# A graph layer with sorted messages: a stated opening order, a small first table, clears in long runs, and blocks stored in pairs

## The chip, the cores and the metric

The kernel runs on one core of a Trainium2 chip. The metric is the device time of one execution in microseconds. Three runs of the kernel before took 1536.56, 1531.3 and 1529.97, median 1531.3.

## The reference

There are 6250 nodes with 128 features, and 100,000 edges, each with a source, a destination and 128 features of its own. The destinations are sorted, the sources are random.

```python
msg_in = jnp.concatenate([x[row], x[col], edge_attr], axis=-1)
h = msg_in @ W + b
# h = layernorm(h) * gamma + beta
msg = jax.nn.relu(h)
out = jax.ops.segment_sum(msg, row, num_segments=x.shape[0])
x = _layernorm(x + out)
```

`row` is the source, `col` the destination. So messages are summed by the random index, and the sorted one is only looked up.

## The kernel before, in words

W has three parts: one for the source, one for the destination, one for the edge. The source and destination parts are computed once per node ("projections", `project(g, k)`, lines 219 to 248, groups of four times 128 nodes): `k = 0` gives xa, kept in SBUF, `k = 1` gives xb, written to the DRAM table xb_d. Both are kept as three bf16 parts that sum to the float32 value.

The edges are cut into 782 tiles of 128, and the tiles into three splits (260, 260, 262). Every edge is assigned to one of 50 blocks by its source (source modulo 50). Each split has a DRAM buffer `sorted`, in which each block has 6 x 128 rows of 132 floats. The work is:

1. **Placement**, `places` (lines 256 to 305). For a chunk of T tiles DVE compares the block numbers with 0 to 49 (L264, 50 x T elements), scans that along the row to count (L266), TensorE adds the counts over the partitions, DVE forms an offset per entry (L280) and a product (L281), TensorE adds both up (L287), and DVE makes `place_i`, the row to which each edge goes. Before it `source_blocks` (L174) computes block numbers from the sources.
2. **Edges**, `edges` (lines 326 to 366), in 196 slots of four tiles. SP loads the edge features eT and the destination offsets db (a pair of slots at a time, `DG = 2`) and a window of 42 rows of the table xb_d; the start row of the window is read into a register of SP (L339). DVE makes a one-hot matrix (L345), TensorE multiplies edge features and window rows (L351, L352), ACT evicts to hs (L354, eight buffers), and GpSimd (POOL) scatters 128 rows of 528 bytes per tile with an indirect DMA (L360). `windows` (L192) makes db's source, drel.
3. **Blocks**, class `Block` (lines 397 to 462), three stages for each of 3 x 50 blocks. `begin` loads the block's rows hl (L411) and makes a one-hot of the source within the block (`ohe`, L415) and its transpose (L422, L423). `middle` adds the source part (L433, L437) and computes the norm (L441 to L449). `end` sums the messages of each node (L457) into acc (L460, L462). A block needs all scatters of its split.
4. **`finish`** (L467) adds x, makes the last layer norm and writes five blocks of the output.

Rows of a block that no edge fills must hold a source number out of range. `clear` (L144) writes such rows into the last two sixths of each block, one DMA per split from ACT's queue.

The program is written in the order opening, then slots of split 0, 1 and 2; a list of side work (projections with `k = 0`, placement of the next split) is taken one by one between the slots, and the blocks of split s are taken between the slots of split s + 1, from its fifth slot on (`LAG`). The blocks of the last split follow at the end. A scheduler in the compiler then orders the instructions of each engine by its own estimate of costs; the opening is given high priority (L503). Each queue and engine runs its instructions strictly in the resulting order. The general path is for inputs that don't fit and isn't run here.

Of the kernel before, what the change touches and what calls it, by code (L numbers as in the profile page):

```python
# [15 lines left out]
P = 128  # L16
# [7 lines left out]
NB, BN = 50, 125  # L24
NPAD = 6400
PT = 4
WN = 42
PIECES = 196
# [3 lines left out]
SPLITS = [(260, 6, 4, [32, 66, 66, 66, 30]), (260, 6, 4, [65] * 4), (262, 6, 4, [66, 66, 66, 64])]  # L32
TMAX = 66
PG = 7
G = 3
# [32 lines left out]
def fast_path(ctx, tc, io, bad_d):  # L68
# [9 lines left out]
    xb_d = dram.tile([3, NPAD, D], BF16, name="xb_d")  # L78
# [10 lines left out]
    proj_pool = early.enter_context(tc.tile_pool(name="proj", bufs=2))  # L89
    src_i = setup.tile([P, TILES], I32, name="src_i")  # L90
    nc.sync.dma_start(src_i, io["srcT"])
    dst_i = setup.tile([HALF, 2, PT * P], I32, name="dst_i")
    nc.sync.dma_start(dst_i, io["dstC"])
    w3 = const.tile([P, 3, D], F32, name="w3")
    nc.scalar.dma_start(w3, io["W"].rearrange("(k p) d -> p k d", p=P))
    base_i = const.tile([1, PIECES], I32, name="base_i")
    nc.scalar.dma_start(base_i, io["base"])
# [3 lines left out]
    for t, v in ((gamma_bc, io["gamma"]), (b_bc, io["b"]), (beta_bc, io["beta"])):  # L101
        nc.scalar.dma_start(t, dram_ap(v, 0, [[0, P], [1, D]]))
# [4 lines left out]
    nc.gpsimd.iota(part_i, pattern=[[1, 1]], base=0, channel_multiplier=1)  # L107
    spare_i = setup.tile([P, TMAX], I32, name="spare_i")
    nc.gpsimd.iota(spare_i, pattern=[[P, TMAX]], base=0, channel_multiplier=1)
    ident = const.tile([P, P], F32, name="ident")  # L110
    make_identity(nc, ident)
    eps = const.tile([P, 1], F32, name="eps")
    nc.vector.memset(eps, LN_EPS)
    iota_row = const.tile([P, P], F32, name="iota_row")
# [5 lines left out]
    ones_h = const.tile([P, P], BF16, name="ones_h")  # L120
    nc.vector.memset(ones_h, 1.0)
# [16 lines left out]

    spare_rows = max(k - f for _, k, f, _ in SPLITS)
    empty = const.tile([P, spare_rows, ROW], F32, name="empty")  # L140
# [3 lines left out]
    def clear(s):  # L144
        _, k, f, _ = SPLITS[s]
        per = k - f
        return nc.scalar.dma_start(
            dram_ap(sorted_d[s], f * P * ROW, [[per * ROW, P], [k * P * ROW, NB], [1, per * ROW]]),
            row_bc(flat(empty[:, :per, :]), NB))
# [4 lines left out]
    nc.vector.tensor_scalar(sgn, gamma_bc, 0.0, 2.0, op0=ALU.is_ge, op1=ALU.mult)  # L154
    nc.vector.tensor_scalar(sgn, sgn, -1.0, None, op0=ALU.add)
    wsum = const.tile([P, 4], F32, name="wsum")
    nc.vector.tensor_reduce(wsum[:, 0:3], w3, axis=AX.X, op=ALU.add)
    nc.vector.tensor_reduce(wsum[:, 3:4], b_bc.unsqueeze(1), axis=AX.X, op=ALU.add)
    wmean = const.tile([P, 4], F32, name="wmean")
    nc.vector.tensor_scalar(wmean, wsum, 1.0 / D, None, op0=ALU.mult)  # L160
    w = const.tile([P, 3, D], F32, name="w")
    for j in (1, 2, 0):
        nc.vector.scalar_tensor_tensor(w[:, j, :], w3[:, j, :], wmean[:, j:j + 1], sgn,
                                       op0=ALU.subtract, op1=ALU.mult)
    bias = const.tile([P, D], F32, name="bias")
    nc.vector.scalar_tensor_tensor(bias, b_bc, wmean[:, 3:4], sgn, op0=ALU.subtract, op1=ALU.mult)
# [7 lines left out]
    def source_blocks(t0, t1):  # L174
        c = slice(t0, t1)
        nc.vector.tensor_copy(src_f[:, c], src_i[:, c])
        nc.vector.tensor_scalar(sloc[:, c], src_f[:, c], 0.5, 1.0 / NB, op0=ALU.add, op1=ALU.mult)
        nc.vector.tensor_scalar(sloc[:, c], sloc[:, c], -0.5, MAGIC, op0=ALU.add, op1=ALU.add)
        nc.vector.tensor_scalar(sloc[:, c], sloc[:, c], -MAGIC, None, op0=ALU.add)
        nc.vector.scalar_tensor_tensor(bkt[:, c], sloc[:, c], -float(NB), src_f[:, c],  # L180
                                       op0=ALU.mult, op1=ALU.add)
        nc.vector.tensor_copy(bkt_h[:, c], bkt[:, c])
        if t1 == TILES:
            for p0 in range(LAST, P, 32):
                nc.vector.memset(bkt_h[p0:p0 + 32, TILES - 1:TILES], 99.0)


    bad = const.tile([P, 3], F32, name="bad")
# [23 lines left out]


    xa = tabs.tile([P, NB, 3 * D], BF16, name="xa")
    acc = tabs.tile([P, NB, ACW], F32, name="acc")
    XG = 4
    n_proj = -(-NB // XG)

    def project(g, k):

        t0 = g * XG
        m = min(XG, NB - t0)
        xT = proj_pool.tile([P, XG * P], F32, name="xT", bufs=4)
        nc.sync.dma_start(xT[:, :m * P], io["xT"][:, t0 * P:(t0 + m) * P])
        ps = psum.tile([P, 4, P], F32, name="hp", bufs=2)
        for j in range(m):
            nc.tensor.matmul(ps[:, j, :], xT[:, j * P:(j + 1) * P], w[:, k, :],
                             start=True, stop=True)
        full = ps[:, :m, :]
        if k == 0:  # L230
            o = xa[:, t0:t0 + m, :]
# [3 lines left out]
        else:  # L235
            xb_t = proj_pool.tile([P, XG, 3 * D], BF16, name="xb")
            o = xb_t[:, :m, :]
        nc.scalar.copy(o[:, :, 0:D], full)
        rest_t = proj_pool.tile([P, XG, D], F32, name="rest")
        rest = rest_t[:, :m, :]  # L240
        nc.vector.tensor_tensor(rest, full, o[:, :, 0:D], op=ALU.subtract)
        nc.scalar.copy(o[:, :, D:2 * D], rest)
        nc.vector.tensor_tensor(o[:, :, 2 * D:3 * D], rest, o[:, :, D:2 * D], op=ALU.subtract)
        if k == 1:
            for i in range(3):
                nc.sync.dma_start(
                    dram_ap(xb_d, i * NPAD * D + t0 * D, [[NB * D, P], [D, m], [1, D]]),
                    o[:, :, i * D:(i + 1) * D])
# [7 lines left out]
    def places(s, t0, T):  # L256
        cap = SPLITS[s][1] * P
# [17 lines left out]
        nc.tensor.matmul(ps[:, NB:2 * NB], ones_h, cnt, start=True, stop=True)  # L275
        at = place_pool.tile([P, NB], F32, name="at")
# [4 lines left out]
        nc.vector.tensor_tensor(sc_v, sc_v, oh_v, op=ALU.mult)  # L281

        sums = psum.tile([P, 512], F32, name="pa")
        for k, (wt, v) in enumerate(((ident_h, sc_v), (ident, far_v))):
            for b in range(0, NB, PG):
# [3 lines left out]
                                 skip_group_check=True)  # L289
        pos_t = place_pool.tile([P, TMAX], F32, name="pos")  # L290
# [4 lines left out]
        nc.vector.scalar_tensor_tensor(place[:, :T], bkt[:, t0:t0 + T], float(cap), pos,  # L295
# [9 lines left out]
        nc.vector.tensor_tensor(place_i[:, t0:t0 + T], place[:, :T], other[:, :T], op=ALU.add)  # L305

# [13 lines left out]
    HS, DG = 8, 2  # L320
# [3 lines left out]
    held = {}  # L324

    def edges(s, q):
        t0 = q * PT
        m = min(PT, TILES - t0)
        if q % DG == 0:
            g = min(DG, PIECES - q)  # L330
            held["eT"] = edge.tile([P, DG * PT * P], F32, name="eT", bufs=3)
            cols = min(g * PT * P, (TILES - t0) * P)
            nc.sync.dma_start(held["eT"][:, :cols], io["eT"][:, t0 * P:t0 * P + cols])
            held["db"] = edge.tile([P, DG * PT * P], BF16, name="db", bufs=3)
            nc.sync.dma_start(held["db"][:, :g * PT * P],
                              dram_ap(drel_d, q * PT * P, [[0, P], [1, g * PT * P]]))
        c0 = q % DG * PT * P
        eT = held["eT"][:, c0:c0 + m * P]
        base = nc.values_load(base_i[0:1, q:q + 1], engines=[mybir.EngineType.SP],  # L339
                              min_val=0, max_val=N - 1,  # L340
                              skip_runtime_bounds_check_because="dst holds node numbers below N")
        win = edge.tile([P, D], BF16, name="win", bufs=6)
        nc.sync.dma_start(win[:3 * WN, :], xb_d[:, bass.ds(base, WN), :])
        oh = edge.tile([P, PT * P], BF16, name="ohd", bufs=3)
        nc.vector.tensor_scalar(oh[:, :m * P], held["db"][:, c0:c0 + m * P], part_w, None,  # L345
                                op0=ALU.is_equal)
# [7 lines left out]
        evict = nc.scalar.copy(hs[:, :m, 0:D], hp[:, :m, :])  # L354
        with tc.issue_after(evict.ins):
# [41 lines left out]
    class Block:  # L397
# [10 lines left out]
        def begin(self):  # L408
            blk, k = late["blk"], self.k
            self.hl = blk.tile([P, KMAX, ROW], F32, name="hl", bufs=4)  # L410
            nc.sync.dma_start(  # L411
                flat(self.hl[:, :k, :]),
                dram_ap(sorted_d[self.s], self.b * k * P * ROW, [[k * ROW, P], [1, k * ROW]]))
            self.ohe = blk.tile([P, KMAX, P], F32, name="ohe", bufs=3)
            nc.vector.tensor_tensor(self.ohe[:, :k, :],  # L415
                                    self.hl[:, :k, D:D + 1].to_broadcast([P, k, P]),
# [84 lines left out]
    n0 = SPLITS[0][3][0]  # L501
    parts0 = place_parts(0)
    with tc.high_priority():  # L503
        source_blocks(0, n0)
        windows()
        for g in range(n_proj):
            project(g, 1)
    parts0.pop(0)()
    source_blocks(n0, TILES)
    clear(0)  # L510
    side = parts0 + [check_windows, cuts]
    side += [lambda g=g: project(g, 0) for g in range(n_proj)]
    side += [lambda s=s: clear(s) for s in range(1, n_split)]
# [23 lines left out]
    LAG = 5  # L537
    for s, (n_tiles, _, _, _) in enumerate(SPLITS):
        p0, p1 = first_tile[s] // PT, -(-first_tile[s + 1] // PT)
        work = side if s == 0 else []  # L540
        if s + 1 < n_split:
            work = work + place_parts(s + 1)
        slots = p1 - p0
        for i in range(slots):
            edges(s, p0 + i)
            n_work = -(-len(work) // (slots - i)) if s else (1 if i % 2 == 0 or len(work) >= slots - i else 0)
            for _ in range(min(n_work, len(work))):
                work.pop(0)()
            if s == 0 and not work and not late:
# [3 lines left out]
            if s > 0 and i >= LAG:  # L553
                q0 = (i - LAG) * NB // (slots - LAG)
                q1 = (i - LAG + 1) * NB // (slots - LAG)
                for _ in range(q1 - q0):
                    step()
    check_rooms()
# [3 lines left out]
    nc.tensor.matmul(total[0:1, 0:3], ones_f, bad, start=True, stop=True)  # L562
# [257 lines left out]
```

## Time and profile before

| what | value |
|---|---|
| median of three runs | 1531.3 us |
| profiled execution | 1529.89 us |
| its span on the core | 1528.1 us |
| mean granted TensorE clock | 0.874 |
| PE, DVE, ACT, POOL busy | 76, 53, 43, 55% of the span |
| DMA in all | 238.46 MB, mean 156 GB/s |

A row of the profile's groups or timelines names the engine, the line, the operation and the tiles (written <- read). A group gives its count, busy time and mean; a timeline gives start and duration in us, and in brackets the idle time ahead of the instruction with what ended it ("issue" means that the engine waited for nothing the profile shows). In the busy slices the span is cut into 40 parts of 38.2 us, and a digit is the busy share in tenths:

```profile
POOL 0000787877878877777777777777777720000000
DVE  6999453432313425445544305545545327777766
```

### The profile page before, as it was taken

What the parts mean: (1) busy time and instruction counts of PE and PEld (TensorE: products, weight loads), DVE (VectorE), ACT (ScalarE), POOL (GpSimd) and SP (SyncE); (2) the same over time, 40 slices, a digit from 0 to 9 for tenths busy, and PEclk for the clock granted to TensorE, in tenths of its full rate; (3) what the DMA queues carried; (4) which work ended last, traced back from release to release, by engine and by line L of the source; (5) the groups of instructions that cost most, each with busy time, mean ns of one, the idle gap of its engine ahead of it and who ended that gap; (6) DMA issues with size and microseconds to landing.
All of it is one profiled execution on the core that took longest, in us unless ns stands there. A gap on an engine that the chain in (4) does not pass through costs nothing.

```text
span 1528.1 us, 26702 instructions
## 1 busy us (share of the span) xinstructions
PE 1162.9 (76%) x8886; PEld 948.1 (62%) x8886; DVE 805.0 (53%) x2127; ACT 658.8 (43%) x2706; POOL 843.7 (55%) x804
## 2 busy tenths in 40 slices
PE   2555565564565479999999839999999848888885
PEld 2233444353343348888888728888888637677674
DVE  6999453432313425445544305545545327777766
ACT  0011212121010026766666516666676526666563
POOL 0000787877878877777777777777777720000000
PEclk9687877765667679999999959999999969999998
DMA  9944534443333346766666447676767223333330
GB/s 322 347 106 104 168 127 136 134 143 113 118 127 111 103 139 208 207 204 205 202 201 198 127 143 226 204 217 196 211 198 204 74 91 99 101 101 94 109 92 31
DMA packets 147179, 238.46 MB, mean 156 GB/s; under 512 B 64050, under 2 KB 84291, under 8 KB 147031
## 3 DMA queue, kind: packets, MB, share of 16 engines
q1 hardware_dynamic: 101924, 163.14, 37.4%
q0 software_dynamic: 25024, 52.85, 9.7%
q10 hardware_dynamic: 20082, 20.67, 4.3%
q8 instruction: 72, 1.18, 0.3%
q14 instruction: 77, 0.62, 0.1%
HBM read 155.11 MB, written 81.47 MB: 155 GB/s over the span
## 4 chain that ended last, share of the span: by engine, by line
PE 46%; POOL 16%; DVE 14%; DMA 12%; issue 9%; ACT 2%; SPq 0%; ACTq 0%; POOLq 0%; DVEq 0%
POOL sorted L360 16%; PE pa L457 11%; PE sel L433 11%; DMA sorted<-hs,place_i 10%; PE sel L437 8%; PE hp L351 7%; PE tr L422 6%; DVE sc L266 2%; DVE ohe L415 2%; PE pa L287 2%; PE hp L352 2%; DVE msg L449 1%; DVE far L280 1%; ACT sq L441 1%; DVE y L477 1%
## 5 line engine op out<-in xcount | busy, mean ns | idle before, releaser
L360 POOL DMA_INDIRECT sorted<-hs,place_i x782 | 841.9, 1077 | 392.8 <-issue 192.4
L351 PE MATMUL hp<-w,eT 128*128 128x128 f32 x1564 | 324.1, 333 | 171.6 <-ACT hs L354 164.8
L351 PEld LDWEIGHTS hp<-w,eT 128*128 128x128 f32 x1564 | 273.7, 219 | 217.0 <-ACT hs L354 189.9
L354 ACT COPY hs<-hp 128x512 f32<-128x512 f32 x196 | 114.7, 585 | 508.3 <-DMA sorted<-hs,place_i 353.0
L441 ACT ACTIVATE sq<-sel 128x128 f32<-128x128 f32 x900 | 251.7, 280 | 128.0 <-PE sel L437 101.8
L433 PE MATMUL sel<-hl,ident 128*128 128x384 f32 x600 | 260.6, 517 | 24.6 <-DVE frstd L484 15.2
L449 DVE SCALAR_TENSOR_TENSOR msg<-sel,rstd,cut 128x128 f32<-128x128 f32 x900 | 247.4, 342 | 1.5
L457 PE MATMUL pa<-msg,ohe 128*128 128x130 f32 x1800 | 244.7, 282 | 2.4 <-DVE msg L449 1.3
L437 PEld LDWEIGHTS <-ohn 128*128 128x128 bf16 x2700 | 182.2, 98 | 92.5 <-issue 58.2
L457 PEld LDWEIGHTS pa<-msg,ohe 128*128 128x128 f32 x1800 | 220.3, 192 | 8.3 <-DVE msg L449 4.8
L437 PE MATMUL sel<-xa,ohn 128*128 128x128 bf16 x2700 | 211.0, 220 | 0.0
L352 PE MATMUL hp<-win,ohd 126*128 126x128 bf16 x782 | 186.0, 239 | 26.0 <-DVE ohd L345 24.4
L441 ACT ACTIVATION_READ_ACCUMULATOR sq<-sel 128x1 f32 x900 | 176.7, 196 | 0.0
L415 DVE TENSOR_TENSOR ohe<-hl,iota_row 128x768 f32<-128x768 f32 x150 | 140.7, 939 | 66.3 <-DMA hl<-sorted 66.3
L423 ACT CAST ohn<-tr 128x384 bf16<-128x384 f32 x300 | 129.3, 482 | 76.0 <-PE tr L422 73.8
L422 PE MATMUL tr<-ident,ohe 128*128 128x128 f32 x900 | 127.7, 279 | 40.5 <-DVE bad_t L565 27.3
L345 DVE TENSOR_SCALAR ohd<-db,part_w 128x512 bf16<-128x512 bf16 x196 | 67.9, 358 | 161.3 <-PE hp L352 141.1
L422 PEld LDWEIGHTS tr<-ident,ohe 128*128 128x128 f32 x900 | 102.0, 144 | 59.1 <-DVE bad_t L565 27.4
L446 DVE RECIPROCAL rstd<-std 128x6 f32<-128x6 f32 x150 | 28.2, 188 | 194.6 <-ACT std L444 193.4
L433 PEld LDWEIGHTS sel<-hl,ident 128*128 128x128 f32 x600 | 92.4, 194 | 29.3 <-issue 17.1
L352 PEld LDWEIGHTS <-ohd 126*128 126x128 bf16 x782 | 85.8, 110 | 28.4 <-DVE ohd L345 25.8
L287 PE MATMUL pa<-far,ident 128*128 128x462 f32 (+4 forms) x208 | 94.6, 593 | 6.9 <-DVE far L280 6.0
(116 smaller groups left out, 692.6 us busy)
## 6 DMA issues: line engine op xcount, KB each, us to landing
hl<-sorted SPq DMA_DIRECT2D x150, 396.0 KB
eT<-in_eT SPq DMA_DIRECT2D x97, 512.0 KB
db<-drel_d SPq DMA_DIRECT2D x98, 256.0 KB
sorted<-empty ACTq DMA_DIRECT2D x3, 6600.0 KB
sorted<-hs,place_i POOLq DMA_INDIRECT x782
win<-xb_d SPq DMA_DIRECT2D x196, 31.5 KB
xT<-in_xT SPq DMA_DIRECT2D x24, 256.0 KB
xb_d<-xb SPq DMA_DIRECT2D x36, 128.0 KB
```

What stands on the lines that cost most here:

```text
L287: nc.tensor.matmul(sums[:, :g * T], wt, flat(v[:, b:b + g, :]), start=(k == 0 and b == 0), stop=(k == 1 and b + PG >= NB), skip_group_chec ...
L351: nc.tensor.matmul(hp[:, j, :], eT[:, at], w[:, 2, :], start=True, stop=False)
L352: nc.tensor.matmul(hp[:, j, :], oh[:3 * WN, at], win[:3 * WN, :], start=False, stop=True)
L360: i = nc.gpsimd.indirect_dma_start(out=sorted_d[s][:, :], out_offset=bass.IndirectOffsetOnAxis(ap=place_i[:parts, t:t + 1], axis=0), in_=h ...
L415: nc.vector.tensor_tensor(self.ohe[:, :k, :], self.hl[:, :k, D:D + 1].to_broadcast([P, k, P]), row_bc(iota_row, k), op=ALU.is_equal)
L422: nc.tensor.transpose(tr[:, j, :], self.ohe[:, j0 + j, :], ident)
L423: nc.scalar.copy(self.ohn[:, j0:j0 + m, :], tr[:, :m, :])
L433: nc.tensor.matmul(sel[:, :m, :], ident, self.hl[:, j0:j0 + m, 0:D], start=True, stop=False)
L437: nc.tensor.matmul(sel[:, j, :], self.ohn[:, j0 + j, :], xa[:, self.b, i * D:(i + 1) * D], start=False, stop=(j == m - 1 and i == 2))
L441: nc.scalar.activation(sq, sel[:, j, :], AF.Square, accum_out=ss[:, j0 + j:j0 + j + 1])
L449: nc.vector.scalar_tensor_tensor(self.msg[:, j0 + j, 0:D], sel[:, j, :], rstd[:, j0 + j:j0 + j + 1], cut, op0=ALU.mult, op1=ALU.max)
L457: nc.tensor.matmul(pa[:, :ACW], self.ohe[:, j, :], self.msg[:, j, :], start=(j == 0), stop=(j == k - 1))
```

## The change

- **Opening in a stated order.** From the opening to the end of split 0's slots the order of PE, DVE, ACT and SP is the order of the program text (`manual_schedule`), not the scheduler's; POOL is not among them. `places` and `project` become steps that are issued one by one. The first chunk of split 0 has 16 tiles instead of 32, then 48, 65, 65, 66; the other chunks of split 0, those of split 1 and all projections but two are issued between the slots of split 0, those of split 2 between the slots of split 1.
- **Two tables.** xb is kept for nodes 0 to 1023 in one table and for 512 to 6655 in another, in node order. Slots 0 to 27 read their windows from the first, for which two projections are enough, the rest from the second. The start rows are computed on DVE (`bases`), and a check of them is added (`check_bases`). One DMA instead of three writes a projection's group.
- **Clears.** Spare rows are cleared in runs of 8 rows (4224 bytes) instead of two (1056). Split 0: five DMAs on POOL's queue. Splits 1 and 2: 25 DMAs each on SP's, one per slot behind that slot's window load.
- **Pairs of blocks.** Rows of two blocks alternate in `sorted`: a row is twice its place, plus its block's parity, plus the pair's start. `source_blocks` makes the start with four more kinds of operation. `begin` loads two blocks with one DMA of 6336 bytes per partition, two buffers instead of four of half the size; each block reads every second row.
- **Loads ahead.** eT and db come for three slots at a time (two buffers instead of three) and four slots ahead, windows three ahead, one-hots two.

```diff
-SPLITS = [(260, 6, 4, [32, 66, 66, 66, 30]), (260, 6, 4, [65] * 4), (262, 6, 4, [66, 66, 66, 64])]
+SPLITS = [(260, 6, 4, [16, 48, 65, 65, 66]), (260, 6, 4, [65] * 4), (262, 6, 4, [65, 65, 66, 66])]
+TABLES = [(0, 1024), (512, 6656)]
+FIRST_TABLE = 28
...
-    def clear(s):
+    def clear(s, p0, n, queue):
         _, k, f, _ = SPLITS[s]
-        per = k - f
-        return nc.scalar.dma_start(
-            dram_ap(sorted_d[s], f * P * ROW, [[per * ROW, P], [k * P * ROW, NB], [1, per * ROW]]),
-            row_bc(flat(empty[:, :per, :]), NB))
+        parts = 2 * (k - f) * P // RUN
+        return queue.dma_start(
+            dram_ap(sorted_d[s], (p0 * k + f) * 2 * P * ROW,
+                    [[RUN * ROW, parts], [2 * k * P * ROW, n], [1, RUN * ROW]]),
+            row_bc(flat(empty[:parts, :, :]), n))
...
-        nc.vector.scalar_tensor_tensor(place[:, :T], bkt[:, t0:t0 + T], float(cap), pos,
+        nc.vector.scalar_tensor_tensor(place[:, :T], pos, 2.0, bkt[:, t0:t0 + T],
                                        op0=ALU.mult, op1=ALU.add)
...
-    HS, DG = 8, 2
+    HS, DG = 8, 3
...
-            self.hl = blk.tile([P, KMAX, ROW], F32, name="hl", bufs=4)
-            nc.sync.dma_start(
-                flat(self.hl[:, :k, :]),
-                dram_ap(sorted_d[self.s], self.b * k * P * ROW, [[k * ROW, P], [1, k * ROW]]))
+            if self.b % 2 == 0:
+                pair = blk.tile([P, 2 * KMAX, ROW], F32, name="hl", bufs=2)
+                nc.sync.dma_start(
+                    flat(pair[:, :2 * k, :]),
+                    dram_ap(sorted_d[self.s], self.b * k * P * ROW,
+                            [[2 * k * ROW, P], [1, 2 * k * ROW]]))
+                late["pair"] = pair
+            pair = late["pair"]
+            self.hl = bass.AP(tensor=pair.tensor, offset=pair.offset + self.b % 2 * ROW,
+                              ap=[list(pair.ap[0]), [2 * ROW, k], [1, ROW]])
...
-    with tc.high_priority():
-        source_blocks(0, n0)
-        windows()
-        for g in range(n_proj):
-            project(g, 1)
-    parts0.pop(0)()
-    source_blocks(n0, TILES)
-    clear(0)
+    first = places(0, 0, n0)
+    order = ExitStack()
+    order.enter_context(tc.manual_schedule(engines={
+        mybir.EngineType.PE, mybir.EngineType.DVE, mybir.EngineType.Activation,
+        mybir.EngineType.SP}))
+    for p0 in range(0, NB // 2, 5):
+        clear(0, p0, 5, nc.gpsimd)
+    source_blocks(0, n0)
+    signs()
+    weights(1, 2)
+    project_a(0, 1)
+    run(first)
+    load_x(2, 1)
+    load_x(3, 1)
+    windows()
+    edge_loads(0)
+    project_b(0, 1)
+    project_a(1, 1)
+    run(first, 2)
+    bases()
+    project_b(1, 1)
+    weights(2, 3)
+    run(first, 2)
+    for q in range(3):
+        edge_window(q)
+    edge_loads(3)
+    edge_hot(0)
+    edge_hot(1)
+    source_blocks(n0, TILES)
+    weights(0, 1)
+    biases()
...
+    steps = {0: place_steps(0) + place_steps(1), 1: place_steps(2), 2: []}
     for s, (n_tiles, _, _, _) in enumerate(SPLITS):
...
         for i in range(slots):
-            edges(s, p0 + i)
+            q = p0 + i
+            edge_loads(q + 4)
+            w_in = edge_window(q + 3)
+            edge_hot(q + 2)
+            edges(s, q)
+            if s + 1 < n_split and 5 <= i < 5 + NB // 2:
+                with tc.issue_after(w_in.ins):
+                    clear(s + 1, i - 5, 1, nc.sync)
+            want = min(n_work, max(min(urgent, i + 1), (i + 1) * n_work // (slots - 4)))
+            for _ in range(want - done_work):
+                work.pop(0)()
+            done_work = want
+            if s == 0:
+                want = min(n_x, 2 * (i + 1))
+                for _ in range(want - done_x):
+                    side_x.pop(0)()
+                done_x = want
...
+        if s == 0:
+            order.close()
```

`steps[0]` has four steps per chunk of split 0 and two per chunk of split 1; `side_x` has two per projection.

## The prediction

> **What bounds the kernel now.** I read the page's busy slices first: POOL is empty for four slices (153 us), then carries 7 or 8 tenths to slice 32, and nothing after it. Then I asked for the busy time of each engine in the stages that the scatter (L360) marks off. Tile 0 of the 782 is scattered at 157.1 us, tile 260 (the first of the second split) at 555.7, tile 520 at 898.5, and the last at 1236.3.
>
> ```profile
> core 0: us, PE busy (x) PEld busy (x) DVE busy (x) ACT busy (x) POOL busy (x), PEclk, DMA share, GB/s
> 157.00:555.00 398.00, 222.60 (x1103) 168.28 (x1101) 143.80 (x208) 61.99 (x168) 318.92 (x260) 0.71 0.41 125
> 555.00:898.00 343.00, 311.38 (x2714) 265.83 (x2712) 160.59 (x514) 205.71 (x864) 263.72 (x261) 0.95 0.63 188
> 898.00:1237.00 339.00, 309.41 (x2756) 268.08 (x2756) 157.87 (x512) 208.50 (x884) 259.13 (x263) 0.95 0.63 188
> 1237.00:1528.10 291.10, 240.51 (x2016) 194.40 (x2016) 200.95 (x690) 165.61 (x761) 0.11 (x1) 0.95 0.30 92
> ```
>
> The same 260 scatters take 398 us in the first stage and 339 in the third. Whom did POOL wait for? The waits of POOL answer:
>
> ```profile
> POOL sorted L360 <- issue: 192.4, 631, 0.3
> POOL sorted L360 <- ACT hs L356: 155.6, 4, 154.7
> POOL sorted L360 <- DMA sorted<-hs,place_i: 22.6, 74, 0.3
> ```
>
> One wait of 154.7 us ahead of the first scatter, and after it never more than the fixed 0.3. So from 157 to 1237 POOL runs back to back, and is the bound. What makes it slower early is in the timelines of POOL and of DVE over the same 10 us:
>
> ```profile
> 207.25 0.96 POOL L360 DMA_INDIRECT sorted<-hs,place_i  x1 [0.30 <-issue]
> 208.52 6.46 POOL L360 DMA_INDIRECT sorted<-hs,place_i  x1 [0.30 <-issue]
> 215.28 0.96 POOL L360 DMA_INDIRECT sorted<-hs,place_i  x1 [0.30 <-issue]
> ```
>
> ```profile
> 207.24 6.97 DVE L266 TENSOR_TENSOR_SCAN sc<-oh 128x3250 bf16<-128x3250 bf16 x1
> 214.14 0.66 DVE L243 TENSOR_TENSOR xa<-rest,xa 128x512 bf16<-128x512 f32 x1
> ```
>
> A scatter that normally takes 0.96 us takes 6.46 and ends when the scan of a placement chunk ends. I went through all 782 scatters so: the long ones lie under the four wide operations of `places` (L264, L266, L280, L281), and a few of 1.2 to 1.7 us under `ohe` (L415). The time of the kernel is therefore four terms, which sum to the span:
> - start of the scatters: 157.1;
> - 782 x (0.957 + 0.304) = 986.1;
> - stretched scatters: 93.8, of which 70.9 under `places`, 21.1 after 565 us under the block work, 1.8 others;
> - from 1237.0 to the end 291.1: the 50 blocks of the last split, which can't start before the last row is scattered.
>
> The profiled execution took 1529.9 with a span of 1528.1; the median of the three runs is 1531.3, 1.4 higher.
>
> **The opening.** Before 157 the trace shows the DMA engines full (323 GB/s in the first 40 us, 347 in the next) with three clears of 6.6 MB, DVE full with five chunks of split 0 and three of split 1 ahead of the first scatter, and 13 projections that must all land before any window is read. The change issues what the first four tiles need and no more: one chunk of 16 tiles, two projections into a small table, one of three clears, and the rest later. How early can the first scatter be?
> - DMA: the clear 6.8 MB, src, dst and four xT 1.9, W and broadcasts 0.4, drel 0.2, eT 0.8, db 0.4, three writes of xb 1.2: 11.7 MB. At the measured 323 to 347 GB/s this is 34 to 36 us, from about 2 us on.
> - The chain: drel is made on DVE at about 13 us (before: 11.8); its write took 7.2 us and the load of db behind it 7.8 (11.81 to 19.06 to 26.83), so db lands near 29. On SP the window loads stand behind the two writes of xb, which wait for DVE at about 22 and queue behind eT; window 0 lands near 33. Then 8 matmuls (2.5), the eviction (0.6), sloc (0.2): 37.
> - POOL now makes the five clears itself. No row of before shows a plain DMA from POOL. The nearest row is a scatter: 0.96 us for 128 rows, so 2.4 for the 320 runs of a clear, 12 for five. Bounds: 0 (they run from 3 us on, while nothing else needs POOL) and +12 (if the DMA engines had to wait for POOL first). The first scatter waits for all five. I take 5, since the DMA engines are busy with other loads meanwhile.
>
> I take 42 for the first scatter, 36 to 57 as bounds: a gain of 115.
>
> **What comes back.** The chunks that were placed before 157 now run beside POOL. Per full chunk (65 or 66 tiles) the trace gives the loss of POOL: scan 6.12 (mean of five), first comparison 2.85 (five), `far` 2.60 (six), product 1.18 (six): 12.75. Before, 5.56 chunks lay in the scatter time (70.9). After, all but the first 16 tiles do: a chunk of 48 and eleven of 65 or 66. The operations themselves take 3.55 + 6.97 + 3.54 + 1.85 = 15.9; the loss is less by 3.2, because each lock partly covers time POOL needed anyway. So the chunk of 48 costs 15.9 x 48/65 - 3.2 = 8.5, the eleven 140.3: together 149, or 78 more than before. In the stated order comparison and scan follow each other directly, and `far` and the product too; before, other work stood between most of them. If POOL gets no turn in between, two covers of 0.8 per chunk are lost: +18 at most; if it gets one, nothing. The one such pair of before (comparison to 153.17, scan from 153.27) leaves a gap of 0.1, as the scan reads what the comparison wrote; so I take POOL to get its turn three times in four: +4.
>
> [...]
>
> **Does POOL stay fed?** Once started it needs four tiles each 5.05 us plus 1.6 of stretch per slot in split 0. The stated order binds SP, ACT, DVE and PE together: on SP the loads of later windows stand behind writes of xb that wait for DVE; on DVE `rest` waits for the copy on ACT. Per slot in split 0: DVE a fraction of a chunk 2.5, one-hot 0.35, a projection with its two waits for ACT (0.68 + 0.85 + 0.68, with the bias once more 1.5) 2.2 to 3.7: 5.1 to 6.6 against POOL's 6.65. PE 2.5 for edges, 1.1 for a projection, 1.2 for placement. Windows are loaded three slots ahead, one-hots two, and hs holds eight: covered, at 0. The chunk of 48 tiles: DVE has its destinations near 62, POOL needs them after 16 tiles, near 70. Without that cover, a slot that waits costs its excess over 6.65: with DVE at 9 us instead, 26 slots x 2.4 = 60.
>
> **Clears of splits 1 and 2, DG 3, lead of the loads.** 25 DMAs of 270 KB on SP in each of two splits, in runs of 4.2 KB instead of 1.1, bytes as before. SP issues them in 0.33 each behind a window load; the DMA share is 0.41 and 0.63 in these stages. 0, bounds -3 and +10.
>
> **Two blocks per load.** hl becomes 75 loads of 792 KB instead of 150 of 396. The buffer of a pair is free only when both its blocks are read, so a load has less time. In the scatter stages before, block 11's load is issued at 611.3 and block 10 is begun at 621.6: 10.3 us for a load. In the tail, hl of block 5 at 1254.3 and ohe of block 4 at 1260.7: 6.4. A lone 396 KB took 3.1 there (1238.31 to 1241.41); 396 KB more at 347 GB/s is 1.2: 4.3. Hidden at 6.4, +1.2 once at the start of the tail. If a load took 7.5, 25 x 1.1 = 28 in the tail. The scatter itself writes the same 528-byte rows; the strided reading of hl by PE and DVE has no row; 0, bounds 0 and +0.2 a block (10 us in the tail).
>
> **Sum.** 42 + 986.1 + 149 + 4 + 23 (block work and others as before) = 1204 for the last scatter, against 1237.0. Then 291.1 + 1.2: span 1496. The execution is 1.8 longer: 1498, to be held against 1529.9; the median would be 1.4 more, which I leave out. The third stage stays balanced: PE ends split 1's blocks 27 us ahead of the last scatter (DVE waits 27.9 us for hl at 1241.4), so small delays of blocks there cost nothing.
>
> **Rivals.**
> - A. The likeliest, as summed: 1498, own range 1478 to 1512. Chance 0.70. Below it reaches if the first scatter comes at 36 and POOL gets turns between locks.
> - B. [...] Chance 0.15; half of it within 0.5% of before.
> - C. Slower: POOL starves in split 0, because the stated order lets DVE's in-line waits for ACT set the slot. Its place is slots 0 to 25, where the projections run. It decides from a DVE slot of 8 us on (26 x 1.35 = 35 eats the gain of 32); at 10 us it is 26 x 3.35 = 87, so 1585. For it: DVE comes to 6.6 of 6.65 in slots with the bias. Against: eight buffers of lead, and in the first stage before the same projections ran beside POOL without one wait. Chance 0.10.
> - D. The tail or the third stage slows by late pairs of blocks, +10 to +28: 1508 to 1526. Chance 0.05. That the change doesn't start the scatters earlier at all I exclude: their inputs are ready by the order itself.
>
> A measurement of this kernel can tell 0.5% (7.7 us) from no change. Faster by more, below 1523.6: A, D and half of B, 0.82; within it 0.07; slower, C with the end of B, 0.11. Range 1476 to 1528.
>
> **What would show it.** First scatter at 36 to 57; POOL's waits otherwise 0.3 each; POOL busy 782 x 0.957 + 176 = 924; scatters of split 0 near 430 us, split 1 near 390, split 2 near 343; last scatter near 1204; tail 291 to 294. Wrong if POOL waits for ACT hs in split 0 (C), if chunks cost near 16 (B), if DVE's ohe waits for hl within the tail (D).

## The result, and the profile after

| | before | after |
|---|---|---|
| median | 1532.07 us (4 runs, 1529.97 to 1536.56) | 1509.79 us (4 runs, 1505.19 to 1512.42) |
| profiled execution, its span | 1529.89, 1528.1 | 1505.19, 1503.4 |
| first scatter, tile 260, tile 520, last | 157.1, 555.7, 898.5, 1236.3 | 49.8, 500.2, 872.9, 1210.6 |
| stretch of scatters, of it under `places` | 93.8, 70.9 | 158.7, 140.8 |
| waits of POOL beyond the fixed 0.3 | none over 0.1 | 17 |

The ratio is 0.985, with a 95% interval of 0.982 to 0.988. The kernel became faster, by 1.5%: of the 32 us that were forecast for the profiled execution, 24.7 came.

The stages marked by the scatters (now L449; before L360) answer to those shown of before. The columns are the same: start and end, length, then the busy time of each engine with its number of instructions, clock, DMA share and rate.

```profile
core 0: us, PE busy (x) PEld busy (x) DVE busy (x) ACT busy (x) POOL busy (x), PEclk, DMA share, GB/s
49.80:500.20 450.40, 242.79 (x1271) 189.42 (x1272) 233.19 (x307) 75.30 (x190) 355.30 (x260) 0.69 0.47 150
500.20:872.90 372.70, 335.50 (x2793) 280.11 (x2791) 208.13 (x558) 204.64 (x864) 293.45 (x261) 0.95 0.59 186
872.90:1211.00 338.10, 308.11 (x2762) 267.63 (x2762) 157.67 (x512) 208.44 (x885) 258.27 (x262) 0.95 0.60 189
1211.00:1503.40 292.40, 241.74 (x2012) 194.91 (x2012) 200.81 (x689) 165.64 (x760) 0.46 (x1) 0.94 0.28 91
```

The third and fourth rows are those of before within 1.3 us. The first stage has become 52 us longer and the second 30: POOL is busy 36 and 30 us longer in them with the same 260 scatters, because DVE now places there. The account against before is: the first scatter 107.3 earlier, 64.9 more stretch, 16.7 of waits, 1.0 in the tail, together 24.7 less.

The waits of POOL show the 16.7:

```profile
POOL sorted L449 <- issue: 194.1, 636, 0.6
POOL sorted L449 <- ACT hs L445: 57.5, 7, 43.2
...
POOL sorted L449 <- DVE xb L303: 3.7, 1, 3.7
```

Of the 57.5 us for hs, 43.2 lie ahead of the first scatter. What remains is in the main four waits, the one for xb among them: 4.1 ahead of tile 4, 3.7 ahead of tile 12, 3.5 ahead of tile 56 (at 151 us) and 5.7 ahead of tile 84 (at 204 us). Before had none of these.

### The profile page after: what moved, and what is told of

It reads as the page before. It is cut to its first block, busy times and chain, and to the rows that moved or that the text cites. A ratio compares the mean times of both kernels' runs of the same rounds, so it can differ in the third digit from the quotient of the medians.

```text
span 1503.4 us, 26307 instructions
## 1 busy us (share of the span) xinstructions
PE 1138.4 (76%) x8890; PEld 941.2 (63%) x8890; DVE 824.0 (55%) x2149; ACT 658.4 (44%) x2706; POOL 913.5 (61%) x809
## 5 line engine op out<-in xcount | busy, mean ns | idle before, releaser
L449 POOL DMA_INDIRECT sorted<-hs,place_i x782 | 907.5, 1160 | 297.3 <-issue 194.1
L439 PE MATMUL hp<-w,eT 128*128 128x128 f32 x1564 | 322.3, 332 | 107.3 <-ACT hs L442 96.8
L552 PE MATMUL pa<-msg,ohe 128*128 128x130 f32 x1800 | 249.2, 283 | 7.1 <-DVE pos L358 4.4
L425 DVE TENSOR_SCALAR ohd<-db,part_w 128x512 bf16<-128x512 bf16 x196 | 68.0, 357 | 135.9 <-PE hp L440 94.6
L557 DVE TENSOR_TENSOR acc<-acc,pa 128x130 f32<-128x130 f32 x100 | 27.8, 278 | 124.5 <-PE pa L552 119.1
```

The costliest lines, as they stand in the source:

```text
L439: nc.tensor.matmul(hp[:, j, :], eT[:, at], w[:, 2, :], start=True, stop=False)
L449: i = nc.gpsimd.indirect_dma_start(out=sorted_d[s][:, :], out_offset=bass.IndirectOffsetOnAxis(ap=place_i[:parts, t:t + 1], axis=0), in_=h ...
L552: nc.tensor.matmul(pa[:, :ACW], self.ohe[:, j, :], self.msg[:, j, :], start=(j == 0), stop=(j == k - 1))
```

## Why the first scatter is at 49.8

The DMAs of SP's queue in the opening (start, duration of the issue, tile):

```profile
13.40 1.28 SPq L236 DMA_DIRECT2D drel_d<-drel  x1
14.72 2.00 SPq L401 DMA_DIRECT2D eT<-in_eT  x1
29.17 0.33 SPq L403 DMA_DIRECT2D db<-drel_d  x1
29.59 7.07 SPq L308 DMA_DIRECT2D xb_d<-xb  x3
43.73 4.49 SPq L415 DMA_DIRECT2D win<-xb_d  x3
```

db can be loaded when drel is in DRAM, and that took from 13.40 to about 29: 15.7 us where before had shown 7.2. The window is issued when the writes of xb have ended, at 43.73. DVE waits for db until 41.35, TensorE for the window until 46.60, and the eviction, sloc and scatter follow by 49.8. What delays both transfers is in the rates of three stretches of 10 us, of after first and of before second (the columns are those of the stages above):

```profile
10.00:20.00 10.00, 2.95 (x20) 2.74 (x18) 7.43 (x21) 1.78 (x3) 0.00 (x0) 1.00 1.01 281
20.00:30.00 10.00, 2.35 (x18) 2.25 (x16) 3.00 (x11) 0.62 (x2) 0.00 (x0) 0.72 1.02 297
30.00:40.00 10.00, 0.77 (x2) 0.50 (x2) 0.00 (x0) 0.00 (x0) 0.00 (x0) 0.50 1.00 258
```

```profile
10.00:20.00 10.00, 3.78 (x16) 3.52 (x17) 10.00 (x23) 1.95 (x3) 0.00 (x0) 1.00 1.05 351
20.00:30.00 10.00, 1.29 (x8) 1.00 (x8) 3.14 (x11) 0.00 (x0) 0.00 (x0) 1.00 1.06 372
30.00:40.00 10.00, 5.87 (x20) 5.06 (x17) 8.04 (x6) 0.00 (x0) 0.00 (x0) 0.98 1.09 351
```

The last two columns matter. In both kernels the 16 DMA engines are busy all the time (share 1.0), but after they move 258 to 297 GB/s, before 351 to 372. Engines that are full at a lower rate mean dearer packets.

## The experiments

All four kernels start from the kernel after. Beside them the kernel before took 1801.75 us (median of 19 runs), where it had taken 1532 beside the result. The record names the chip of the experiments and not that of the result; I take it for another one and call it the second chip. In the profiles from it TensorE, DVE and ACT stop again and again, with no releaser that the profile knows; of TensorE, in the middle of a block's matmuls:

```profile
PE sel L536 <- issue: 19.1, 17, 2.6
```

This is from 1040 to 1200 us of `clears_gated`; in the same 160 us of the kernel after, beside the result, TensorE has one wait of 0.7 and no other. Why that chip stops so isn't settled. The slots come late there in every stage, so POOL waits 269 to 304 us in all. The kernel after itself was not run on that chip. So I compare the four with each other and with before as run beside them, and rest on terms that the stops touch little: the opening (in `edges_ahead`, whose opening is that of the kernel after, SP's DMAs start within 0.4 us of those in the result's run, and three of the four kernels have the first scatter within 1 us of 49.8) and the stretch.

The waits are those of POOL beyond the fixed 0.3, in us.

| | median, ratio to before there | first scatter | tile 260 | last | stretch under `places`, other | waits of POOL, split 0, 1, 2 |
|---|---|---|---|---|---|---|
| `clears_gated` | 1794.37, 0.997 [0.993, 1.001] | 50.0 | 528.6 | 1487.7 | 138.9, 31.8 | 46, 123, 116 |
| `clear_twice` | 1823.91 (one run) | 80.7 | 551.8 | 1528.7 | 135.9, 24.6 | 45, 137, 122 |
| `edges_ahead` | 1793.92, 0.997 [0.994, 1.000] | 50.2 | 531.3 | 1493.2 | 135.4, 29.4 | 47, 133, 114 |
| `chunks33` | 1731.87, 0.962 [0.953, 0.971] | 50.8 | 489.2 | 1440.3 | 106.6, 31.0 | 32, 120, 117 |

### `clears_gated`: is it the wait for drel?

```diff
-    for p0 in range(0, NB // 2, 5):
+    for p0 in (0, 5):
         clear(0, p0, 5, nc.gpsimd)
...
         nc.sync.dma_start(drel_d.rearrange("(p h) e -> p (h e)", h=2), flat(drel))
+        gate = setup.tile([HALF, 2], BF16, name="gate")
+        nc.gpsimd.tensor_copy(gate, drel[:, :, 0])
+        for p0 in (10, 15, 20):
+            clear(0, p0, 5, nc.gpsimd)
```

> The kernel after, with three of split 0's five clears held back on POOL until DVE has made drel (about 13 us); bytes, placement and everything else as before. Theory S (the first scatter is late because the write of drel and the load of db stand in DMA engines filled by the clears): the write of drel takes about 8 us instead of 15.7, db lands near 32 instead of 41.4, and the first scatter comes near 42 (when the held-back clears land) instead of 49.8; the time falls by about 7. Rival (the first scatter is set by DVE's order or by the writes of xb and the window, not by drel): the first scatter stays at 48 to 50.

The DMAs of SP's queue:

```profile
13.59 1.31 SPq L236 DMA_DIRECT2D drel_d<-drel  x1
14.94 2.10 SPq L405 DMA_DIRECT2D eT<-in_eT  x1
25.29 0.33 SPq L407 DMA_DIRECT2D db<-drel_d  x1
25.71 7.07 SPq L312 DMA_DIRECT2D xb_d<-xb  x3
43.82 4.49 SPq L419 DMA_DIRECT2D win<-xb_d  x3
```

db is issued 3.9 earlier than in the result's run and lands at 36.66 instead of 41.35 (32 was forecast), and the writes of xb are issued 3.9 earlier too. But the window is issued at 43.8, as in the result's run, and the first scatter stays at 50.0. Theory S in the form written down, with drel and db as what decides, is refuted. The rival named the writes of xb and the window as what decides, and the first scatter stayed where it put it. The writes of xb, issued earlier, took as much longer until the window could be issued. That points to the sum of bytes, not to the order.

### `clear_twice`: is it the bytes?

```diff
-    for p0 in range(0, NB // 2, 5):
+    for p0 in list(range(0, NB // 2, 5)) * 2:
         clear(0, p0, 5, nc.gpsimd)
```

> The kernel after, with split 0's spare rows cleared twice in the opening: 6.8 MB more, same result. Theory S: the DMA engines are full until the first scatter, so 6.8 MB at 340 GB/s put it back by about 20 us, to near 70. Rival (DMA latency of the chain drel, db, window alone, or POOL's generation of descriptors at 0.7 each): no more than 4 us later.

The first scatter comes at 80.7, 30.5 later than in `edges_ahead`, whose opening up to there is that of the kernel after. 6.76 MB more in 30.5 us are 222 GB/s. (Each second clear writes rows that a first one writes. The second five are issued apart, one between 10 and 20 us, two between 20 and 30, one each in the next two stretches of 10, each taking POOL 0.68 to 0.88 us; the DMA engines stay full all the same, with shares of 0.99 to 1.03 from 10 to 70 us.) It is the bytes, as S said, and each costs more than the 340 GB/s behind S's 20 us. How much more, the DMA queues show. Between 48 and 72 us the opening consists almost of clears alone (packets, MB, share of the time of 16 engines); the second fence is ACT's queue before, from 44 to 84:

```profile
q0 software_dynamic: 1120, 4.52, 91.0%
```

```profile
q10 hardware_dynamic: 10756, 11.32, 88.4%
```

A packet of the new clears has 4.04 KB and takes 0.910 x 24 x 16 / 1120 = 0.312 us of an engine, 12.9 bytes per ns. A packet of the old ones has 1.05 KB and takes 0.053 us, 20.0 per ns. In the result's own run, from 12 to 42, the clears show 15.2 (5.34 MB in 73.3% of 16 engines). With 16 engines that is 243 against 320 GB/s: split 0's 6.76 MB take 27.8 us of all engines instead of 21.1, so 6.7 more (an estimate from these rates). The forecast had the bytes through 34 to 36 us after the start at 2, so at 36 to 38; measured, the window was issued behind the last write of xb at 43.7.

Three properties differ: the runs are four times as long, they come from 64 partitions instead of 128 (`parts` is 2 x 2 x 128 / 8), and the queue is POOL's instead of ACT's. The trace of the kernel after separates two of them, for its 50 later clears are the same transfer on SP's queue. Between 173.0 and 174.4 us the packets of one of them have nothing beside them but small ones (first two lines); between 546.42 and 546.55 twelve packets of another start (last two):

```profile
DMA packets 131, 0.28 MB, mean 203 GB/s; under 512 B 67, under 2 KB 67, under 8 KB 131
q1 hardware_dynamic: 131, 0.28, 91.9%
...
DMA packets 17, 0.05 MB, mean 390 GB/s; under 512 B 5, under 2 KB 5, under 8 KB 17
q1 hardware_dynamic: 17, 0.05, 96.8%
```

The packets of 512 bytes and more are the clear's. In the first stretch they are 64, of at most 0.919 x 1.4 x 16 / 64 = 0.32 us each: as dear as from POOL's queue. In the second they are 12, of 0.968 x 0.13 x 16 / 12 = 0.17 us: 25 bytes per ns. So POOL's queue isn't needed for the high price, and a long run out of 64 partitions isn't dear by itself. The price comes when many such packets are under way: by the packet records of the same trace, of all 3200 later ones those with on average fewer than eight under way took 0.164 us in the middle, those with fourteen or more 0.329, twice as long.

What is left are the 64 partitions. That they set the price is my best reading, not shown by a test: a clear in long runs from 128 partitions was not run. Measured are the 30.5 us for a second clear of 6.76 MB, and 224 GB/s in all DMA between 45 and 70 us, with the engines full (share 1.01).

### `edges_ahead`: is it TensorE behind placement?

The first of the four waits of POOL had looked like this: TensorE stands at the count of a placement chunk, behind it a projection and the edge matmuls of the next slot. From TensorE's timeline of the kernel after, and the scatter that waits, from POOL's:

```profile
59.24 0.22 PE L337 MATMUL pa<-cnt,before 128*128 128x50 bf16 x1 [10.45 <-DVE cnt L335]
...
59.33 2.05 PE L281 MATMUL hp<-w,xT 128*128 128x128 f32 x8
61.18 0.63 PE L439 MATMUL hp<-w,eT 128*128 128x128 f32 x2
```

```profile
64.83 0.96 POOL L449 DMA_INDIRECT sorted<-hs,place_i  x1 [4.11 <-ACT hs L445]
```

The other three stand in the same way behind the sums of a chunk (L352), which TensorE does in one piece: ahead of tile 12 from 68.96 to 75.91, of tile 56 from 138.90 to 146.82, of tile 84 from 191.78 to 199.78. A projection and the edge matmuls follow, and the eviction stands on ACT behind both copies of the projection.

```diff
-            edge_loads(q + 4)
-            w_in = edge_window(q + 3)
-            edge_hot(q + 2)
-            edges(s, q)
+            edge_loads(q + 4 + AHEAD)
+            w_in = edge_window(q + 3 + AHEAD) or w_in
+            edge_hot(q + 2 + AHEAD)
+            edges(q + AHEAD)
+            scatters(s, q)
```

`AHEAD` is 2; the first two slots' edges come ahead of the loop, and `scatters` is the second half of `edges`, which stays in its place.

> The kernel after, with the matmuls, eviction and loads of a slot issued two slots ahead of its scatters (the scatters stay where they are). Theory P (POOL's four waits of 3.5 to 5.7 us in split 0 come from the stated order: TensorE stands at placement matmuls ahead of the next slot's edge matmuls): the four waits vanish, split 0's scatters take about 17 us less, the time falls by 12 to 17. Rival (DVE's in-line waits for ACT in the projections set a slot's pace): the waits move two slots later and their sum stays within 5 us of 17.

The waits ahead of tiles 4 and 12 are gone. But POOL then waits 7.4 us ahead of tile 16 and 12.4 ahead of tile 64, and split 0 loses 47 us to waits, as much as in the two kernels above (45 and 46); its time is that of `clears_gated`. For tile 16 these three lines, of POOL, ACT and DVE, belong together:

```profile
85.79 0.96 POOL L456 DMA_INDIRECT sorted<-hs,place_i  x1 [7.35 <-issue]
```

```profile
74.18 0.20 ACT L447 COPY hs<-sloc 128x4 f32<-128x4 f32 x1
```

```profile
84.83 0.21 DVE L371 TENSOR_TENSOR place_i<-place,other 128x48 int32<-128x48 f32 x1
```

The profile names no releaser ("issue"), but the times do: the messages of slot 4 were complete at 74.4, its destinations at 85.0, and the scatter begins 0.8 later. Tile 16 is the first of the chunk of 48. Its product ends on DVE at 72.5; its sums on TensorE at 79.7, at a granted clock of 0.79; then DVE stands in line at a projection that waits for ACT, and only then comes the step that makes `place_i`. For tile 64 it is the same: its destinations were complete at 177.4, and it was scattered at 178.1. In the kernel after, tile 16 was scattered at 84.8 too, and tile 64 at 161.5. There the 48 destinations were complete at 81.3, ahead of need, but only because POOL came late: without its two waits (4.11 + 3.70, 7.2 beyond the fixed part) it would have come to tile 16 at about 77.6 (an estimate) and waited there for the destinations. So the lead of the edges only exchanges one wait for another. The place of the waits follows TensorE's placement matmuls, as P had it; but behind them stands the chain of a placement chunk through DVE, TensorE and DVE, with a projection between each two steps. Theory P is refuted as a cure. The rival named the projections' waits for ACT and a sum that stays; the sum stayed that of the other kernels on this chip, but the new waits lie at the starts of chunks and not two slots later, so neither theory had the place. Whether the placement's chain alone, with no projections between, would be early enough was not tried.

### `chunks33`: what does a chunk cost POOL?

```diff
-SPLITS = [(260, 6, 4, [16, 48, 65, 65, 66]), (260, 6, 4, [65] * 4), (262, 6, 4, [65, 65, 66, 66])]
-TMAX = 66
+SPLITS = [(260, 6, 4, [16, 30, 30, 30, 30, 31, 31, 31, 31]), (260, 6, 4, [32, 32, 32, 32, 33, 33, 33, 33]),
+          (262, 6, 4, [32, 32, 33, 33, 33, 33, 33, 33])]
+TMAX = 33
```

> The kernel after, with placement in chunks of 30 to 33 tiles (16 first) instead of 48 to 66: twice as many placement operations, each half as long. Theory L (every wide operation of DVE takes from POOL its duration less about 0.8 us, which POOL needs anyway): 23 chunks x (7.95 - 4 x 0.8 to 1.0) = 91 to 110 us of stretch under placement instead of 141; the time falls by 30 to 50, unless TensorE and DVE starve POOL with the added small operations. Rival, the full lock: the stretch stays at about 141, the time within 10 us of the kernel after.

The stretch under placement is 106.6 us, against 135 to 139 in the other three kernels: 29 to 32 less, inside the 91 to 110 of theory L and far from the rival's 141. One comparison and scan show how. First DVE and POOL in the kernel after (66 tiles), then in `chunks33` (31 tiles):

```profile
215.60 3.59 DVE L327 TENSOR_TENSOR oh<-bkt_h,iota_h 128x3300 bf16<-128x3300 bf16 x1
219.22 7.03 DVE L329 TENSOR_TENSOR_SCAN sc<-oh 128x3300 bf16<-128x3300 bf16 x1
```

```profile
215.72 4.30 POOL L449 DMA_INDIRECT sorted<-hs,place_i  x1 [0.31 <-issue]
220.33 6.70 POOL L449 DMA_INDIRECT sorted<-hs,place_i  x1 [0.30 <-issue]
```

```profile
220.56 1.77 DVE L328 TENSOR_TENSOR oh<-bkt_h,iota_h 128x1550 bf16<-128x1550 bf16 x1
222.36 3.39 DVE L330 TENSOR_TENSOR_SCAN sc<-oh 128x1550 bf16<-128x1550 bf16 x1
```

```profile
220.59 2.57 POOL L450 DMA_INDIRECT sorted<-hs,place_i  x1 [0.31 <-ACT hs L446]
223.47 3.05 POOL L450 DMA_INDIRECT sorted<-hs,place_i  x1 [0.30 <-issue]
```

With 66 tiles DVE is busy 10.62 in the two operations, and the two scatters are 4.30 + 6.70 - 2 x 0.96 = 9.08 too long: 1.54 is covered. With 31 tiles DVE is busy 5.16, the scatters are 3.70 too long: 1.46 is covered. The cover of the pair is the same 1.5 at both lengths: each of the four scatters ends 0.8 after the operation beside it, whatever that one took. So operations of half the length are covered twice as well for the same work. Over all wide operations beside the scatters the cover is 0.96 per operation in the kernel after (48 operations of 186.9 us in all, 140.8 lost) and 0.91 in `chunks33` (96 of 194.4, 106.6 lost).

The kernel's median is 62 us below those of `clears_gated` and `edges_ahead`, more than the forecast 30 to 50. Of the profiled runs (that of `clears_gated` was its fastest) it is 47 in the time and in the last scatter: 32 of it stretch under placement, 14 fewer waits in split 0. The ratio to before, 0.962, is the lowest of all kernels here. Against the kernel after this version wasn't run on one chip; by the terms it would win about 30 of stretch there (an estimate from the differences above).

## Why the prediction was right, and where not

The sign, the bound and the mechanism held: POOL stays the bound, the early start (107 of the forecast 115) is partly paid back by placement beside the scatters, and the last split and its blocks stay as they were. The forecast was 1498.0 for the profiled execution, which took 1505.19; the other runs reached up to 1512, which no trace here explains. Term by term:

- **First scatter: 42 forecast, 49.8 measured, +7.8.** The step that failed is "At the measured 323 to 347 GB/s this is 34 to 36 us". To count the bytes was right, as `clear_twice` shows; the rate was not. I took it from clears out of 128 partitions in 1 KB runs on ACT's queue and gave it to clears out of 64 in 4 KB runs on POOL's. The chain beside it ("db lands near 29", window near 33) took latencies from an opening with other queues; it came to 41.4 and 46.6, each transfer waiting in full engines. POOL's own part, taken at 5, was not it: the five clears were issued by 6.6 us, at 0.7 each. So the chain of 37 was 12.8 short, and the 5 that POOL didn't need made the error look smaller.
- **"Does POOL stay fed?": 0 forecast, 17 measured.** The step compared the sum of DVE's work in a slot with POOL's 6.65 us, and found cover in buffers. But at the start no buffer is full yet, and what counts there is not a sum per slot but the time through a chain that visits DVE, TensorE and ACT in turn, each in a fixed order. The term "1.2 for placement" on PE is such a mean: the sums of a chunk come in one piece of 6.9 to 8.0 us, more than POOL's 6.65 for a slot, with the next slot's matmuls behind it. "DVE has its destinations near 62" shows it too: they were complete at 81.3. Rival C had the place right (slots 0 to 25) and the size too large: 17 and not 35 to 87, for the slots between and after the four were fed.
- **Stretch: 149 + 4 + 23 forecast, 140.8 + 17.9 measured, -17.** The chunk of 48 cost 7.5 and not 8.5, each of the eleven others 12.1 in the mean and not 12.75. The 4 for joined operations were not needed: in the lines above POOL gets its turn between comparison and scan. Had the wide operations cost POOL their full time, it would have been 187 (the 48 of them took 186.9). The rows of before were a good guide to the price: by them 12.75 a chunk. They even show the cover: the scatter at 207.25 begins with the scan and passes in 0.96, and the one behind it ends at 214.98, 0.8 after the scan and not with it, as the prediction reads it. What the prediction calls a lock is no more than such rows: beside the scan of 7.03 above, the scatter took 6.70 instead of 0.96. What holds POOL there isn't shown. Rival B, with chunks near 16, falls with this: no run shows such a chunk.
- **Pairs of blocks, clears on SP, tail: 292.3 forecast, 292.4 measured.** DVE waits once for hl (30.2 at the start of the tail; 27.9 before), and not again in the tail beyond what it did before. D didn't occur.

The errors, +7.8, +17 and -17, leave 7: a nearly right sum whose parts are further off than the whole. That waits and stretch cancel is luck. By stages it shows: split 0 took 450 against a forecast of 430, split 1 373 against 390, split 2 338 against 343.

Open remain: how much of the gain is the stated order's, since no kernel without it was run; how the kernel after stands to before on the second chip; and whether chunks below 30 tiles go on paying, as each brings its small operations with it.

## What to carry to other kernels

Here a wide operation of DVE cost POOL its duration less a cover that didn't grow with it (in the mean 0.96 with chunks of 48 to 66 tiles, 0.91 with 30 to 33), so where POOL is the bound, try such work in shorter pieces; halving it won about 30 us of 137 here, and further was not tried. Before pricing an opening by bytes over rate, take the rate from transfers of the same shape (partitions, run, queue), not from another transfer that also filled the engines (12.9 to 15.2 against 20.0 bytes per ns here). A lead of buffers feeds an engine only after it has been built up (the four waits of POOL in the kernel after, 3.5 to 5.7 us, lay at tiles 4 to 84): for the first items follow one item through all its engines in their stated order.

## What the runs showed of the hardware that I had not expected

- With all DMA engines busy, clears of 4.04 KB packets from 64 partitions on POOL's queue moved 12.9 to 15.2 bytes per ns of an engine, clears of 1.05 KB packets from 128 partitions on ACT's queue 20.0. The same packets as the first took 0.17 us in a short burst from SP's queue and up to 0.32 when 64 of them went with little beside them. Long packets were not slow everywhere: in the tail of the kernel after, the loads of hl, xs and the stores of y moved 23.90 MB in 29.0% of 250 us (20.6 per ns, 4.3 KB a packet), before in 31.6% (18.9, 2.7 KB).
- POOL issued a plain DMA of 320 runs in 0.7 us, less than the 0.96 of an indirect one with 128 rows.
- The kernel before took 1532 us beside the result and 1802 beside the experiments. Of the kernel after and its variants, the opening and the stretch under placement agreed in both places (140.8 us beside the result, 135 to 139 in the three variants with the same chunks); in the second, TensorE, DVE and ACT stopped at points that the profile ascribes to nothing.
